# Stage 2 of a two-layer cross-attention kernel: the two folding steps of a pair are placed beside its products, and the output bias is added on VectorE

## The chip, the cores and the metric

One core of a Trainium2 chip runs the whole program. The metric is the device time in microseconds (us), the median over executions of one build; lower is better. Engine names are those of the profile: PE is the matrix engine (TensorE), PEld its weight loads, DVE is VectorE, ACT is ScalarE, POOL is GpSimd, SP is the sync engine, which here issues most of the DMAs.

## The reference

Two cross-attention layers follow one another over x, 4 x 1024 tokens of width 1024, with a context of 64 rows for each batch. Everything is float32.

```python
# layer 0: 32 heads of 32, 8 key/value heads, post-norm
q = x @ Wq + bq;  k = ctx @ Wk + bk;  v = ctx @ Wv + bv
attn = softmax(q k / sqrt(32) + mask)
x1 = layernorm((attn v) @ Wo + bo + x) * gamma + beta
# layer 1: 16 heads of 64
a = layernorm(ctx);  Q = x1 @ Wq1.T;  K = a @ Wk1.T;  V = a @ Wv1.T
y = x1 + tanh(gate) * (softmax(Q K / 8, masked) V) @ Wo1.T
```

Layer 1 has only 64 keys for each batch, so the kernel folds its weights: for each batch and head, Wq1 and K become one matrix `ad` (1024 x 1024, queries straight to scores), and V and Wo1 become one matrix `bd` (probabilities straight to the output).

## The kernel before, in words

The work goes in stages. Stage 1 makes layer 0's queries, scores, softmax and head outputs, and folds `ad`. **Stage 2**, which the change touches, multiplies the head outputs by Wo (`w_o`), adds the residual x and the bias bo, normalizes, writes x1 to DRAM, and folds `bd` on the side. Stage 3 does layer 1 with the folded matrices.

Stage 2 runs over 16 pairs of 128-row tiles. Pair 0 is done at the end of stage 1; the loop over `pair in range(1, NPAIR)` does the others. The product of a pair (256 x 1024 times 1024 x 1024) is done by a seven-product scheme of Strassen's kind, in `products`. Its seven steps, by bank, left block and right block, are

- step 0: X, A11 B11; step 1: X, S2 T2; step 2: V, S3 T3; step 3: X, S1 T1; step 4: X, S4 B22; step 5: V, A22 N4; step 6: W, A12 B21.

X, V and W are PSUM banks of the pool `wx` (4 buffers). X gathers four products one after another and V two; after every product its bank, as it then stands, is added on DVE to a quarter of the pair's residual rows `r` (line 455). So step 1 may write to X only when the DVE add of step 0 has read it, and step 4 only after the add of step 3. A product has four matmuls of 128 x 128 by 128 x 512; each shows as two PE instructions, so a product is "x8". In the trace's names, step 0 is `wo_B,o`, step 1 `wo_T,S`, step 2 `wo_T,o`, steps 3 and 4 `wo_B,S`, step 5 `wo_N,o` and step 6 `wo_B,o` again.

`project(a, w, r, fill, ...)` runs the seven steps and, after each, `ceil(len(fill)/7)` functions of the list `fill`. Into `fill` go, for a pair:

- `close_rows(pair - 1, r)`: for each of the two 128-row tiles of the pair before: two `bn_stats` (line 292), `bn_aggr` and an add (297, 298) with a square root on ACT (299), a reciprocal and a `scalar_tensor_tensor` (302, 306), a second one (309), and the store of x1 (1053). That is 12 functions.
- for pairs 1 to 8, `folded_values(vT, wch, pair - 1)`: two functions `keys(0)` and `keys(1)`. With 12 functions ahead of them and two after each step, they come in program order after step 6; in pair 1, which has two more functions ahead and three after each step, after steps 4 and 5.
- for pairs 13 to 15, sums of layer 1's first weight and transposes of x1.

One `keys` function makes, for two batches, a part of `bd`:

```python
for n in range(2):
    banks = two()                       # one of two "big" buffers: two PSUM banks
    for e in range(2):                  # rows 0..63 and rows 64..127 of the array
        nc.tensor.matmul(banks[e], vT[q, c, sub_ap(bp)], wch[q, n*512:(n+1)*512], ...)   # L924
    for e in range(2):
        nc.scalar.activation(st[:, e, n*512:(n+1)*512], banks[e], AF.Copy, scale=tanh_gate)  # L929
# then two DMAs of st to bd on SP (L933)
```

So a `keys` function is four matmuls of 64 rows, in two couples e = 0 and e = 1 that lie on different halves of the array, or eight PE instructions ("x8"), and four ACT evictions of 128 x 512.

`load_outputs(pair + 1)` (line 942 on), called at the head of a pair's turn, loads the next pair's head outputs `o` and its two residual tiles `r` on SP, and adds bo to each `r` on POOL (line 958), ahead of all products of that pair. `left_out` (lines 429 to 432), called by `tail` ahead of step 5, makes the next pair's left blocks on DVE.

The order in which an engine runs its instructions is set when the program is built: a planner goes through them in the order of the code, but where an engine would stand idle it takes the next instruction in that order that it holds to be ready. The trace shows it: in pairs 2 to 8 the first matmul of step 2 (`wo_T,o` x2) runs ahead of step 1 (`wo_T,S` x8). `tc.keep_in_program_order` pins an instruction behind the one that was written before it for its engine; the first `bn_stats` of a tile is pinned so, behind the add of the step that comes before it in the code.

Of the kernel before, what the change touches and what calls it, by code (L numbers as in the profile page):

```python
# [11 lines left out]
ALU = mybir.AluOpType  # L12
# [59 lines left out]
def tile_two_cross_attentions(  # L72
# [25 lines left out]
    nc = tc.nc  # L98

    def sub_ap(t):  # L100
        return slice(t * P, (t + 1) * P)
# [15 lines left out]
    def wx():  # L117
        return ps_wx.tile([P, 512], F32, tag="wx", name="wx")
# [14 lines left out]
    def open_pool(stack, name, bufs, side="left"):  # L133
        return stack.enter_context(tc.tile_pool(name=name, bufs=bufs, side=side, reuse_waits="tile"))
# [68 lines left out]
    def right_weight(w, tag, name, turned=False):  # L203
        r, loads = right_loads(w, tag, name, turned)
        run(loads)
        return r, right_sums(r)

    def run(steps):
        for s in steps:
            s()  # L210
# [179 lines left out]
    def two():  # L390
        b = big()
        return [b[:, 0:512], b[:, 512:1024]]
# [42 lines left out]
    def products(a, w, r, bias=None, tail=None):  # L435

        fresh = set()
        banks = {}  # L440

        def product(name, s, m, first, last):
            if first:
                banks[name] = wx()
            for k in range(HK):
                nc.tensor.matmul(  # L446
                    banks[name], a[s][:, k, :], w[m][:, k, :],
                    start=first and k == 0, stop=last and k == HK - 1, skip_group_check=True,
                )

        def add(u, n, name):
            bank = banks[name]
            at = r[u][:, n * 512 : (n + 1) * 512]
            if bias is None or (u, n) in fresh:
                nc.vector.tensor_tensor(at, bank, at, ALU.add)  # L455
            else:
                fresh.add((u, n))
                at = at.rearrange("p (h s) -> p h s", s=S)
                nc.vector.tensor_tensor(  # L459
                    at, bank.rearrange("p (h s) -> p h s", s=S),  # L460
                    bias.unsqueeze(1).to_broadcast([P, 512 // S, S]), ALU.add,
                )

        def step(name, s, m, first, last, u, n):
            if s == "A22" and tail:
                tail()
            product(name, s, m, first, last)
            add(u, n, name)

        order = [  # L470
            ("X", "A11", "B11", True, False, 0, 0),
            ("X", "S2", "T2", False, False, 1, 0),
            ("V", "S3", "T3", True, False, 1, 1),
            ("X", "S1", "T1", False, False, 1, 1),
            ("X", "S4", "B22", False, True, 0, 1),
            ("V", "A22", "N4", False, True, 1, 0),
            ("W", "A12", "B21", True, True, 0, 0),
        ]
        return [lambda o=o: step(*o) for o in order]

    def project(a, w, r, fill, bias=None, tail=None):

        share = -(-len(fill) // 7)
        for step in products(a, w, r, bias, tail):
            step()
            for _ in range(min(share, len(fill))):
                fill.pop(0)()

# [371 lines left out]
    steps = query_steps(0, rows)  # L860
# [16 lines left out]
    def chunk(w, k, name):  # L877
        t = wpool.tile([P, H], F32, tag="wb", name=f"{name}_{k}")
        nc.sync.dma_start(out=t, in_=w[sub_ap(k), :])
        return t  # L880
# [34 lines left out]
    def folded_values(vT, wch, c):  # L915


        def keys(bp):
            st = wpool.tile([P, 2, H], F32, tag="wb", name=f"b_{c}_{bp}")
            for n in range(2):  # L920
                banks = two()
                for e in range(2):
                    q = slice(e * S, (e + 1) * S)
                    nc.tensor.matmul(  # L924
                        banks[e], vT[q, c, sub_ap(bp)], wch[q, n * 512 : (n + 1) * 512],
                        start=True, stop=True,
                    )
                for e in range(2):
                    nc.scalar.activation(  # L929
                        st[:, e, n * 512 : (n + 1) * 512], banks[e], AF.Copy, scale=tanh_gate[:, 0:1]  # L930
                    )
            for b2 in range(2):
                nc.sync.dma_start(  # L933
                    out=bd[bp * 2 + b2, sub_ap(c), :].rearrange("(e s) o -> s e o", e=2),
                    in_=st[b2 * S : (b2 + 1) * S],
                )

        return [lambda bp=bp: keys(bp) for bp in range(2)]

    def load_o(pair, pool, tag="o2"):  # L940
        o = pool.tile([P, KC, 2 * P], F32, tag=tag, name=f"o2_{pair}")
        load = nc.sync.dma_start(out=o, in_=oTd[pair])
        if pair < 2:
            tc.keep_in_program_order(load)
        return o

    def load_outputs(pair):
        o = load_o(pair, o2pool) if pair > 1 else second if pair else load_o(0, early)
        r = []
        for u in range(2):  # L950
            t = pair * 2 + u
            ru = (rpool.tile([P, H], F32, tag="r", name=f"r_{t}") if pair
                  else early.tile([P, H], F32, tag="r", name=f"r_{t}", bufs=2))
            load = nc.sync.dma_start(out=ru, in_=x[sub_ap(t), :])
            if not pair:
                tc.keep_in_program_order(load)
            if pair:
                nc.gpsimd.tensor_tensor(ru, ru, bo_sb, ALU.add)  # L958
            r.append(ru)
        return o, r  # L960

# [86 lines left out]
    vT = fold.tile([P, KC, B * S], F32, tag="kvT", name="vT")  # L1048
    nc.sync.dma_start(out=vT, in_=vTd)

    def close_rows(pair, r):
        def last(u):
            nc.sync.dma_start(out=x1[pair][sub_ap(u), :], in_=r[u])

        steps = []
        for u in range(2):
            steps += normalize_steps(
                r[u], EPS0, f"0_{pair * 2 + u}", True, (gamma0_sb, beta0_sb)
            ) + [lambda u=u: last(u)]
        return steps  # L1060
# [3 lines left out]
    def load_x1(pair):  # L1064
        xq = xqpool.tile([P, 2 * NQ, QW], F32, tag="xq", name=f"xq1_{pair}")
        load_quarters(xq, x1[pair])
        return xq

    def turn_x1(pair, xq, pool=None, tag="xT"):
# [11 lines left out]
    wch = chunk(wo1, 0, "wo1")  # L1081
# [7 lines left out]
    values()  # L1089
    open_stage()  # L1090
    _, ahead_r = load_outputs(1)
    run(first)

    fill = [
        lambda u=u: nc.vector.tensor_tensor(first_rows[u], first_rows[u], bo_sb, ALU.add) for u in range(2)
    ]
    fill += close_rows(0, first_rows)
    for pair in range(1, NPAIR):
        r, a = ahead_r, ahead_a
        if pair + 1 < NPAIR:  # L1100
            ahead_o, ahead_r = load_outputs(pair + 1)
        if pair <= KC:
            ahead_w = chunk(wo1, pair, "wo1") if pair < KC else None
            fill += folded_values(vT, wch, pair - 1)
            wch = ahead_w
        if pair == KC + 2:
            w_a, w_a_sums = right_weight(ad[0], "wb", "a0", True)
        if pair in (NPAIR - 3, NPAIR - 2):
            fill += w_a_sums[0:2] if pair == NPAIR - 3 else w_a_sums[2:4]
        if pair == 3:  # L1110
            early_cm.close()
            xTpool = open_pool(last_cm, "x1T", 1)
            lxpool = open_pool(last_cm, "leftx", 1)
            xqpool = open_pool(last_cm, "x1q", 1)
        if pair == NPAIR - 4:
            xq = load_x1(1)
        if pair == NPAIR - 3:
            fill += turn_x1(1, xq)

        def tail():  # L1120
            nonlocal ahead_a
            if pair + 1 < NPAIR:
                ahead_a = left_out(ahead_o, lpool, f"0_{pair + 1}")
            else:
                turned[2]()

        project(a, w_o, r, fill, tail=tail)
        fill = close_rows(pair, r)
        if pair == NPAIR - 2:
            xq = load_x1(0)  # L1130
            turned = turn_x1(0, xq, o2pool, "o2")
            fill = turned[:2] + fill
# [78 lines left out]
    for pair in range(NPAIR):  # L1211
        r = []
        for u in range(2):
            ru = rpool.tile([P, H], F32, tag="r", name=f"r1_{pair}_{u}")
            nc.sync.dma_start(out=ru, in_=x1[pair][sub_ap(u), :])
            r.append(ru)
        fill = []
# [79 lines left out]
```

## Time and profile before

| | us |
|---|---|
| median of 3 runs | 1914.9 (1913.46 to 1915.07) |
| the profiled execution's own time | 1915.11 |
| its span, first to last instruction | 1913.3 |
| stage 2's loop, first product of pair 1 to first product of stage 3 | 719.8 to 1130.0 |
| PE busy over the span | 1868.9 (98%) |
| DVE / ACT / POOL busy | 1292.1 (68%) / 427.9 (22%) / 179.1 (9%) |
| the 30 adds of bo on POOL (line 958) | 78.5, mean 2.625 each |
| the two adds of bo on DVE, for pair 0 (line 1095) | 2.5, mean 1.226 each |
| a DVE add of a bank to `r` (line 455) | 0.686 |
| an ACT eviction of `keys` (line 929) | 0.687 |

Start times in the trace are microseconds from the span's start. The time outside the span is 1.8 us. "x8" in a line of the timeline is a run of eight instructions of one kind, with the time that they cover; "[0.97 <-DVE r L455]" behind a line is how long the engine stood idle before it and what ended that. The times of PE runs overlap a little, so that the distance from one start to the next is the better measure of what a run costs.

### The profile page before, as it was taken

How to read it: one execution, taken by the hardware profiler on the slowest of the kernel's cores; microseconds unless marked ns; L12 is line 12 of the kernel's file. 1: busy time of each engine (PE TensorE's matmuls, PEld its weight loads, DVE VectorE, ACT ScalarE, POOL GpSimd, SP SyncE). 2: the span in 40 equal slices, each digit the busy share in tenths (PEclk: the TensorE clock that was granted, in tenths of full speed). 3: DMA queues.
4: the chain of work that ended last, by engine and by line, in shares of the span. 5: the costliest groups of instructions: out<-in, count | busy, mean ns of one | idle time of the engine just before them, and what ended most of it. 6: DMA issues, size and time to landing. Idle time of an engine off the chain costs nothing.

```text
span 1913.3 us, 17522 instructions
## 1 busy us (share of the span) xinstructions
PE 1868.9 (98%) x6096; PEld 880.0 (46%) x6096; DVE 1292.1 (68%) x1582; ACT 427.9 (22%) x1396; POOL 179.1 (9%) x212
## 2 busy tenths in 40 slices
PE   8999999999998899999999999999999999999999
PEld 7744444444455653343344444444444444444444
DVE  3425589789878985575568778557665766576653
ACT  1101575666536751212100001000000000000000
POOL 0016011111100103121113100000000000000000
PEclk9999999999999899999999999999999999999999
DMA  8996599899878966567473363466656565657421
GB/s 276 184 222 192 158 253 247 253 252 261 252 186 275 302 234 207 188 207 238 164 218 138 121 141 90 110 165 158 150 143 165 150 158 143 165 142 165 121 88 44
DMA packets 220745, 350.54 MB, mean 183 GB/s; under 512 B 26992, under 2 KB 146160, under 8 KB 215664
## 3 DMA queue, kind: packets, MB, share of 16 engines
q1 hardware_dynamic: 152896, 242.44, 45.8%
q0 software_dynamic: 15216, 60.83, 10.5%
q10 hardware_dynamic: 52544, 46.14, 8.8%
q8 instruction: 48, 0.79, 0.2%
q14 instruction: 41, 0.34, 0.1%
HBM read 207.53 MB, written 141.82 MB: 183 GB/s over the span
## 4 chain that ended last, share of the span: by engine, by line
PE 82%; DVE 8%; DMA 5%; issue 2%; ACT 2%; POOL 0%; SPq 0%; DVEq 0%; POOLq 0%; ACTq 0%
PE wx L446 59%; PE wx L576 14%; PE big L680 2%; DMA pq<-p 2%; PE big L924 1%; PE wx L379 1%; PE big L379 1%; DVE s L684 1%; PE big L759 1%; DMA p<-s 1%; DMA q<-qTd 1%; DVE s L715 1%; DVE mx L691 1%; DVE sm L711 1%; DMA o<-oTd 1%
## 5 line engine op out<-in xcount | busy, mean ns | idle before, releaser
L455 DVE TENSOR_TENSOR r<-wx,r 128x512 f32<-128x512 f32 x224 | 153.5, 686 | 230.1 <-PE wx L446 215.3
L698 ACT ACTIVATE s<-s,mx 128x64 f32<-128x64 f32 x488 | 162.8, 335 | 74.9 <-DVE mx L691 70.7
L502 ACT ACTIVATE s<-s 128x1024 f32<-128x1024 f32 x32 | 33.7, 1057 | 651.7 <-DVE s L501 651.7
L459 DVE TENSOR_TENSOR s<-wx,key_bias 128x512 f32<-128x512 f32 x64 | 44.1, 690 | 136.7 <-PE wx L446 136.7
L446 PE MATMUL wx<-wo_B,S 128*128 128x512 f32 x256 | 117.1, 600 | 1.5 <-DVE r L455 1.5
L576 PE MATMUL wx<-xT,wq_S 128*128 128x512 f32 x256 | 116.5, 598 | 0.8 <-ACT z L587 0.8
L446 PE MATMUL wx<-b_B,pT 128*128 128x512 f32 x256 | 115.8, 593 | 0.6 <-ACT pT L414 0.6
L446 PE MATMUL wx<-b_B,S_p 128*128 128x512 f32 x256 | 116.0, 596 | 0.0
L446 PE MATMUL wx<-a_B,xT 128*128 128x512 f32 x256 | 115.4, 592 | 0.0
L446 PE MATMUL wx<-a_B,S_x 128*128 128x512 f32 x256 | 115.3, 593 | 0.1
L576 PE MATMUL wx<-xB,wq_A 128*128 128x512 f32 x256 | 115.1, 597 | 0.0
L446 PE MATMUL wx<-wo_B,o 128*128 128x512 f32 x256 | 114.8, 596 | 0.0
L958 POOL TENSOR_TENSOR r<-r,bo 128x1024 f32<-128x1024 f32 x30 | 78.5, 2625 | 313.8 <-DMA r<-in_x_dram 159.4
L684 DVE TENSOR_TENSOR s<-big,m 128x1024 f32<-128x1024 f32 x64 | 77.4, 1215 | 28.4 <-PE big L680 26.8
L680 PEld LDWEIGHTS big<-kv,q 64*128 64x128 f32 x1024 | 71.1, 195 | 48.3 <-issue 39.9
L698 ACT ACTIVATION_READ_ACCUMULATOR s<-s,mx 128x1 f32 x488 | 91.4, 187 | 0.0
L680 PE MATMUL big<-kv,q 64*128 64x128 f32 x1024 | 82.6, 292 | 2.6 <-DMA q<-qTd 2.6
L419 DVE STREAM_TRANSPOSE pT<-pq 128x1024 f32<-128x1024 f32 x66 | 78.0, 1219 | 3.3 <-DMA pq<-p 3.3
L446 PEld LDWEIGHTS wx<-wo_B,S 128*128 128x128 f32 x256 | 47.1, 190 | 67.7 <-issue 51.2
L715 DVE TENSOR_TENSOR s<-s,sm 128x1024 f32<-128x1024 f32 x64 | 77.0, 1216 | 0.9
L446 PEld LDWEIGHTS wx<-wo_B,o 128*128 128x128 f32 x256 | 47.8, 190 | 63.5 <-issue 62.3
L446 PEld LDWEIGHTS wx<-a_B,S_x 128*128 128x128 f32 x256 | 48.5, 190 | 62.0 <-issue 58.4
(162 smaller groups left out, 2903.5 us busy)
## 6 DMA issues: line engine op xcount, KB each, us to landing
p<-s POOLq DMA_DIRECT2D x19, 1024.0 KB, 8.1
pq<-p POOLq DMA_DIRECT2D x76, 256.0 KB, 6.0
xq<-in_x_dram SPq DMA_DIRECT2D x64, 256.0 KB, 10.2
q<-qTd SPq DMA_DIRECT2D x32, 512.0 KB, 7.4
oTd<-oT ACTq DMA_DIRECT2D x32, 512.0 KB, 7.4
ad<-a POOLq DMA_DIRECT2D x16, 1024.0 KB, 8.9
o<-oTd SPq DMA_DIRECT2D x16, 1024.0 KB, 5.1
r<-in_x_dram SPq DMA_DIRECT2D x32, 512.0 KB, 5.3
```

The costliest lines, as they stand in the source:

```text
L379: nc.tensor.matmul(ps[:, 0:256], w[k // HK, c // HK][:, k % HK, sub_ap(c % HK)], ct[:, k, :], start=(k == 0), stop=(k == KC - 1),)
L419: return nc.vector.transpose(dst.rearrange("p k (u i) -> p k u i", i=Q), t[:, :, k0 * Q : k1 * Q].rearrange("p u (k j) -> p k u j", j=Q),)
L446: nc.tensor.matmul(banks[name], a[s][:, k, :], w[m][:, k, :], start=first and k == 0, stop=last and k == HK - 1, skip_group_check=True,)
L455: nc.vector.tensor_tensor(at, bank, at, ALU.add)
L459: nc.vector.tensor_tensor(at, bank.rearrange("p (h s) -> p h s", s=S), bias.unsqueeze(1).to_broadcast([P, 512 // S, S]), ALU.add,)
L502: nc.scalar.activation(s, s, AF.Exp)
L576: nc.tensor.matmul(bank, w_q[a][:, k, sub_ap(i)], rows[b][:, k, :], start=first and k == 0, stop=last and k == HK - 1, skip_group_check=True,)
L680: nc.tensor.matmul(ps[:, at : at + P], q[on, c * 4 + g, :], k0bd[on, b, c, :], start=True, stop=True,)
L684: nc.vector.tensor_tensor(quarters[:, :, c * 8 : (c + 1) * 8], ps.rearrange("p (k a l) -> p a k l", a=NQ, l=Q), mask.rearrange("p e (h l) ...
L698: nc.scalar.activation(heads[:, e, k], heads[:, e, k], AF.Exp, bias=mx[:, e, k : k + 1], accum_out=sm[:, e, k : k + 1],)
L715: nc.vector.tensor_tensor(heads[:, e], heads[:, e], wide(sm[:, e]), ALU.mult)
L958: nc.gpsimd.tensor_tensor(ru, ru, bo_sb, ALU.add)
```

## The change

1. The functions of `folded_values` leave `fill`. `project` takes a table `beside`, from the index of a step to a function, and calls it right after that step, ahead of the functions of `fill`. `keys(0)` is called after step 1, `keys(1)` after step 4, in pairs 1 to 8.
2. The adds of bo on POOL in `load_outputs` are gone. Instead `close_rows` begins with two DVE adds of bo, one for each tile, after all products of the pair have been added to `r`; the two that pair 0 had already on DVE are now these.

`fill` so has 14 functions in nearly every pair (two after each step). The first `bn_stats` of the first tile now comes in the code after step 1, that of the second after step 4 (before, after steps 0 and 3).

```diff
-    def project(a, w, r, fill, bias=None, tail=None):
+    def project(a, w, r, fill, bias=None, tail=None, beside={}):
         share = -(-len(fill) // 7)
-        for step in products(a, w, r, bias, tail):
+        for i, step in enumerate(products(a, w, r, bias, tail)):
             step()
+            if i in beside:
+                beside[i]()
             for _ in range(min(share, len(fill))):
                 fill.pop(0)()
...
-            if pair:
-                nc.gpsimd.tensor_tensor(ru, ru, bo_sb, ALU.add)
...
-        steps = []
+        steps = [lambda u=u: nc.vector.tensor_tensor(r[u], r[u], bo_sb, ALU.add) for u in range(2)]
...
-    fill = [
-        lambda u=u: nc.vector.tensor_tensor(first_rows[u], first_rows[u], bo_sb, ALU.add) for u in range(2)
-    ]
-    fill += close_rows(0, first_rows)
+    fill = close_rows(0, first_rows)
...
+        beside = {}
...
-            fill += folded_values(vT, wch, pair - 1)
+            beside = dict(zip((1, 4), folded_values(vT, wch, pair - 1)))
...
-        project(a, w_o, r, fill, tail=tail)
+        project(a, w_o, r, fill, tail=tail, beside=beside)
```

## The prediction

> **What bounds the kernel now.** I read the page first: its busy times, then the chain that ended last.
>
> ```profile
> PE 1868.9 (98%) x6096; PEld 880.0 (46%) x6096; DVE 1292.1 (68%) x1582; ACT 427.9 (22%) x1396; POOL 179.1 (9%) x212
> ...
> PE 82%; DVE 8%; DMA 5%; issue 2%; ACT 2%; POOL 0%; SPq 0%; DVEq 0%; POOLq 0%; ACTq 0%
> ```
>
> PE holds the end almost everywhere, so the question in stage 2 is what lies between two products on PE. Next, the timeline of PE over one pair (pair 4; pairs 2 to 8 are alike).
>
> ```profile
> 809.32 3.70 PE L446 MATMUL wx<-wo_B,o 128*128 128x512 f32 x8
> 812.85 1.02 PE L446 MATMUL wx<-wo_T,o 128*128 128x512 f32 x2
> 813.86 3.70 PE L446 MATMUL wx<-wo_T,S 128*128 128x512 f32 x8
> 817.39 2.74 PE L446 MATMUL wx<-wo_T,o 128*128 128x512 f32 x6
> 819.97 3.60 PE L446 MATMUL wx<-wo_B,S 128*128 128x512 f32 x8
> 823.40 1.02 PE L446 MATMUL wx<-wo_N,o 128*128 128x512 f32 x2
> 824.35 3.70 PE L446 MATMUL wx<-wo_B,S 128*128 128x512 f32 x8
> 827.88 2.74 PE L446 MATMUL wx<-wo_N,o 128*128 128x512 f32 x6
> 830.46 3.60 PE L446 MATMUL wx<-wo_B,o 128*128 128x512 f32 x8
> 833.99 1.99 PE L924 MATMUL big<-wo,vT 64*128 64x512 f32 x8
> 836.53 2.28 PE L924 MATMUL big<-wo,vT 64*128 64x512 f32 x8 [0.56 <-ACT b L929]
> ```
>
> The next pair starts at 838.74, so the pair takes 29.42 us. Two things are to be seen. First, the two `keys` steps together take 838.74 - 833.99 = 4.75 us, because the second waits for ACT to empty the two big buffers. Second, between steps 0 and 1 and between steps 3 and 4 X is being read by DVE, and each such **gap** lasts 1.01 or 0.95 us (812.85 to 813.86, 823.40 to 824.35). It is not idle: the planner has put the first matmul of the next product there (x2, worth 2 x 0.43 = 0.86), and that product is short by it later (x6, 2.58).
>
> Third, pair 1, the one place of the trace where a `keys` step is written right behind step 4, as the change writes both.
>
> ```profile
> 731.43 3.60 PE L446 MATMUL wx<-wo_B,S 128*128 128x512 f32 x8
> 734.95 1.12 PE L924 MATMUL big<-wo,vT 64*128 64x512 f32 x2
> 736.01 3.70 PE L446 MATMUL wx<-wo_B,S 128*128 128x512 f32 x8
> 739.64 1.98 PE L924 MATMUL big<-wo,vT 64*128 64x512 f32 x6
> 741.55 3.70 PE L446 MATMUL wx<-wo_N,o 128*128 128x512 f32 x8
> 745.18 1.99 PE L924 MATMUL big<-wo,vT 64*128 64x512 f32 x8
> ```
>
> Here the gap was filled with the first matmul of `keys(0)`, as it is the next in the code, and step 5 has all its eight instructions afterwards. What is left of `keys(0)` (x6) takes 741.55 - 739.64 = 1.91 us, while a whole `keys` step takes the same: 747.10 (the next PE row) - 745.18 = 1.92. Six cost what eight cost because the halves e = 0 and e = 1 run side by side: in the whole step each half has four instructions at 0.43; with one matmul of half 0 gone, half 1 still has four. **A matmul of `keys` in the gap saves nothing, one of a product saves 0.86 us.**
>
> Fourth, the timeline of all engines at a POOL add.
>
> ```profile
> 1062.89 2.35 POOL L958 TENSOR_TENSOR r<-r,bo 128x1024 f32<-128x1024 f32 x1 [12.87 <-DVE r L306]
> 1062.94 3.38 DVE L309 SCALAR_TENSOR_TENSOR r<-r,rstd,beta 128x1024 f32<-128x1024 f32 x1
> ...
> 1066.98 3.27 PE L446 MATMUL wx<-wo_B,S 128*128 128x512 f32 x7 [0.63 <-DVE r L455]
> ```
>
> A DVE instruction that takes 1.28 us elsewhere takes 3.38 beside the POOL add, and here PE waits for the add queued behind it.
>
> **The change, part by part.** *The `keys` steps, pairs 2 to 8.* Removed: 4.75 us at the end of the pair, of which about 0.9 is waiting for ACT. Added, by pair 1's rows: step 0 before a `keys` matmul 3.52 (734.95 - 731.43), gap 1.06 (736.01 - 734.95), step 1 3.63, x6 1.91, step 2 whole 3.54 (as 779.92 to 783.46, a product after `keys`), then the same again for steps 3, 4, `keys(1)` and 5, and step 6 3.44: 2 x (3.52 + 1.06 + 3.63 + 1.91 + 3.54) + 3.44 = 30.76. Before, the seven pairs from 750.53 to 956.41 took 29.41 each. So +1.35 a pair, **+9.4 us** for seven. The bounds: if both gaps keep a product's matmul and both `keys` steps run whole, a pair is 3.44 + 1.01 + 3.63 + 1.92 + 2.6 + 3.43 + 0.95 + 3.63 + 1.92 + 2.6 + 3.44 = 28.57, or -0.84 (-5.9 in seven); if a gap takes both matmuls of one couple, the rest is x4, some 1.06 instead of 1.91, and with both gaps so the pair is 29.06 (-0.35). I take 30.76, as the row it rests on is the same code at the same place.
>
> ACT has its four evictions 0.7 us apart after the second half of each `keys` step (2.42 us in pair 1), then 10 us until the next: no wait for a buffer is left. The square root of line 299 may queue behind them for up to 2.4 us; DVE waits for it, and the adds that matter are those of steps 0 and 3, several us later. The four DMAs to bd go on SP as before, two after each `keys`; SP is in order, and behind them stand the stores of x1 and the loads of `o` and `r`. They take 5.4 us for four (837.66), now 2.7 twice. The load of `o` goes out when step 6 frees its buffer (834.09) and is used 20.7 us later (854.83); that distance is five products and two `keys` after as before. `r`, landed 5.2 us after its issue, has no POOL add behind it any more and waits for nothing new. Step 6 of the pair before must end, then DVE's store of x1 (one step later in the code) before a buffer of `r` is free; 6 buffers are three pairs, so this has over 20 us.
>
> *Pair 1.* It took 750.53 - 719.79 = 30.74 with one step split already and a wait of 0.97 at 725.31, behind a POOL add (DVE 724.57, idle 1.80 <-POOL). That wait goes (`r` landed at 721.9, step 0 ends at 723.3), the second split comes: 30.76, **0**. With the wait left it would be +1.
>
> *bo off POOL.* 30 adds of 2.625 us leave POOL, where nothing is queued behind them, and 30 of 1.226 come to DVE, 2.45 us a pair. DVE was busy 16.9 of 29.4 us in pairs 5 and 6, so there is room. The place that counts is ahead of step 0's add: the adds of bo can start after step 6's add, and in pairs without `keys` DVE stood idle 2.80 us there (before 984.68, 1009.17 and 1059.33). 2.45 fits with 0.35 to spare, and one of the two can go a product earlier. I take 0; if it doesn't fit, see rival 3. The lock goes: PE's step 3 came 0.59, 0.58 and 0.79 us late in pairs 11 to 13 (starts of 1016.62, 1041.61 and 1066.98 against the x6 before them plus 2.58), each behind a DVE instruction stretched by POOL: **-2.0 us**. DVE is nearly full there (31.2 of 32.0 us from 1009 to 1041, stretches included), so up to +1.5 may come back; 0 to be gained elsewhere, because other stretched instructions held up no product. In these pairs the first `bn_stats` now comes after step 1's add and the second tile's after step 4's, so DVE's long chain ends near the add of step 3; that is the +1.5.
>
> The Trainium skill, SBUF — State Buffer, section "Who interferes with whom", says that a DVE instruction with two SBUF inputs and a GpSimd instruction that reads SBUF lock each other out for a whole instruction. The 3.38 beside 2.35 agrees. By that rule alone DVE would get all of its lost time back; by the rows only three stretches reach PE.
>
> TensorEngine Tiling (Array Packing), section "Key Properties", says that a change of tiling mode drains the engine, which speaks against spreading: the two `keys` steps now stand in four places, not one. The rows have the price as about 0.1 us at each change (3.52 against 3.43), and it is in the sum. The page gives no time for it.
>
> *The end of stage 2.* Pair 15's closing runs beside the first scores, DVE busy without a break from 1130 to 1143. It becomes 2.45 us longer, but PE fills there with x4 runs of later products. 0, at most +2.
>
> **Sum**: +9.4 + 0 - 2.0 = +7.4 on the profiled 1915.1, or 1922.5. The profiled execution is 0.2 above the median of the runs, so this stands for the median too.
>
> **Rivals.**
> 1. *One gap of two is filled by a couple* (DVE's new adds make step 0's add later, the planner sees it and puts both halves there). The pair is 30.76 - 0.85 = 29.91, +0.5; 3.5 - 2.0 gives **1916.6**. For it: DVE is fuller ahead of step 0. Against: the filler was x2 in every gap of pairs 1 to 10.
> 2. *The other side: the `keys` steps run whole and the products keep the gaps.* Then the wait for ACT goes and nothing is lost: -5.9 - 2.0, **1907**. It decides if the planner holds the `keys` matmul not ready in the gap (its weights' chunk or its buffer late), so that step 2's or 5's comes first. For it: the gaps of pairs 2 to 8. Against: there no `keys` step was next in the code; where one was, it was taken.
> 3. *A new wait*: an add of bo starts just ahead of the end of step 0 and the add of step 0, which frees X, waits for it, up to 1.2 us in 15 pairs. On average half of it, +9: **1932**. Against: 2.80 against 2.45.
>
> **Chances.** Forecast 0.69, rival 1 0.11, rival 2 0.14, rival 3 0.06. The range takes the forecast with its bounds (+1 for pair 1, +1.5, +2 and a little of rival 3) and rival 1 with 2 us either way: 1914 to 1928, some 0.8. A measurement of this kernel can tell about 0.2% (3.8 us) from no change. Faster by more is rival 2 with rival 1's best corner, 0.15; within, rival 1 with a mixed forecast, 0.12; slower 0.73.
>
> **What would show it.** In the PE timeline of a pair 2 to 8: `big` x2 in both gaps, x6 after steps 1 and 4, steps 2 and 5 as x8, and 30.8 us from pair to pair. Line 306 and 309 means near 1.28 instead of 1.46 and 1.52, and no PE wait near 1016, 1042 and 1067. ACT's evictions never ahead of a PE wait. The prediction is wrong if the gaps hold x2 of a product or x4 or x8 of `keys`, or if DVE's add of step 0 starts more than 0.3 us after step 0.

## The result, and the profile after

The changed kernel takes 1919.8 us (median of 6 runs, 1917.13 to 1921.85), the kernel before 1914.6 (6 runs, 1913.14 to 1915.49). The ratio is 1.0026, with a 95% interval of 1.0014 to 1.0039: **slower by 5.2 us**. The profiled execution took 1920.84, its span is 1919.1. So the spans of the two profiled executions differ by 5.8 us.

The page's busy times and the chain that ended last, of the changed kernel:

```profile
PE 1881.0 (98%) x6096; PEld 881.9 (46%) x6096; DVE 1303.2 (68%) x1612; ACT 427.2 (22%) x1396; POOL 100.6 (5%) x182
...
PE 85%; DVE 7%; DMA 4%; issue 1%; ACT 1%; POOL 0%; DVEq 0%; SPq 0%; POOLq 0%; ACTq 0%
```

On the chain, PE has 85% where it had 82, ACT and issue 1 each where they had 2: waits went, and the time still grew. POOL lost its 78.5 us of adds and DVE has 30 instructions more. PE runs the same 6096 instructions and is busy 12.1 us longer, so no work was added to it: the same instructions lie less favourably. How is seen in the timeline of PE over half a pair of the changed kernel (pair 3; pairs 2, 5, 6, 7 and 8 look the same; columns: start, time covered, line, tiles, size, count):

```profile
785.58 1.12 PE L927 MATMUL big<-wo,vT 64*128 64x512 f32 x2
786.63 3.70 PE L446 MATMUL wx<-wo_T,S 128*128 128x512 f32 x8
790.26 1.98 PE L927 MATMUL big<-wo,vT 64*128 64x512 f32 x6
792.17 3.70 PE L446 MATMUL wx<-wo_T,o 128*128 128x512 f32 x8
795.71 3.60 PE L446 MATMUL wx<-wo_B,S 128*128 128x512 f32 x8
```

The gap between steps 0 and 1 (785.58 to 786.63) now holds the first matmul of `keys(0)`. The rest of that function, x6, still takes 1.91 us (792.17 - 790.26), and step 2 is whole, x8, 3.54. The wait of `keys(1)` for ACT, 0.56 before, is gone.

The other thing to be seen is DVE. Groups by shape, stage 2 of the changed kernel (busy us, mean ns | idle before):

```profile
L306 DVE SCALAR_TENSOR_TENSOR r<-r,mv,gamma 128x1024 f32<-128x1024 f32 x31 | 39.5, 1275 | 0.0
L1056 DVE TENSOR_TENSOR r<-r,bo 128x1024 f32<-128x1024 f32 x32 | 39.1, 1222 | 0.8
L309 DVE SCALAR_TENSOR_TENSOR r<-r,rstd,beta 128x1024 f32<-128x1024 f32 x30 | 38.5, 1282 | 0.7
```

The same view of the kernel before has, for lines 309 and 306:

```profile
L309 DVE SCALAR_TENSOR_TENSOR r<-r,rstd,beta 128x1024 f32<-128x1024 f32 x31 | 47.5, 1532 | 0.6
L306 DVE SCALAR_TENSOR_TENSOR r<-r,mv,gamma 128x1024 f32<-128x1024 f32 x31 | 45.3, 1460 | 0.0
```

Lines 306 and 309 fell from 1460 and 1532 ns to 1275 and 1282, since no POOL instruction lies beside them any more. The 32 adds of bo cost DVE 39.1 us.

To find where 5.8 us come from, I cut both spans at the first product of pairs 1, 2 and 9 and of stage 3:

| us | before | after | difference |
|---|---|---|---|
| ahead of pair 1 | 719.79 | 720.45 | +0.66 |
| pair 1 | 30.74 | 30.85 | +0.11 |
| pairs 2 to 8 | 205.88 | 214.41 | +8.53 |
| pairs 9 to 15 | 173.55 | 170.15 | -3.40 |
| stage 3 to the end | 783.34 | 783.24 | -0.10 |

In six of pairs 2 to 8 the changed kernel takes 30.75 us; in pair 4 it takes 29.91. **The pairs with `keys` lose 8.5 us, the pairs without win 3.4 back.**

### The profile page after: what moved, and what is told of

Read it like the earlier page. It is cut to its first block, busy times and chain, and to the rows that moved or that the text cites. A ratio compares the mean times of both kernels' runs of the same rounds, so it can differ in the third digit from the quotient of the medians.

```text
span 1919.1 us, 17488 instructions
## 1 busy us (share of the span) xinstructions
PE 1881.0 (98%) x6096; PEld 881.9 (46%) x6096; DVE 1303.2 (68%) x1612; ACT 427.2 (22%) x1396; POOL 100.6 (5%) x182
## 4 chain that ended last, share of the span: by engine, by line
PE 85%; DVE 7%; DMA 4%; issue 1%; ACT 1%; POOL 0%; DVEq 0%; SPq 0%; POOLq 0%; ACTq 0%
PE wx L446 61%; PE wx L579 14%; PE big L927 2%; PE big L683 2%; PE wx L379 1%; PE big L379 1%; DVE s L687 1%; PE big L762 1%; DMA p<-s 1%; DVE mx L694 1%; DVE s L718 1%; DMA pq<-p 1%; DMA q<-qTd 1%; DMA o<-oTd 1%; DVE sm L714 1%
## 5 line engine op out<-in xcount | busy, mean ns | idle before, releaser
L932 ACT ACTIVATE b<-big,tanh_gate 128x512 f32<-128x512 f32 x64 | 39.7, 682 | 198.8 <-PE big L927 122.6
L446 PEld LDWEIGHTS wx<-a_B,xT 128*128 128x128 f32 x256 | 48.6, 190 | 61.2 <-issue 60.5
```

The source lines that it names most:

```text
L446: nc.tensor.matmul(banks[name], a[s][:, k, :], w[m][:, k, :], start=first and k == 0, stop=last and k == HK - 1, skip_group_check=True,)
L932: nc.scalar.activation(st[:, e, n * 512 : (n + 1) * 512], banks[e], AF.Copy, scale=tanh_gate[:, 0:1])
```

## The experiments

**The theories.** *Filler theory* (mine): the loss is that a matmul of `keys` takes the place of a product's matmul in the gap, and that half of a couple taken alone saves nothing later. Then the loss hangs on which instruction is next in program order when the gap opens, and not on the steps being apart. *Spreading theory*: the loss is that the 64-row matmuls stand in four places between the products instead of in one. *DVE theory*: the loss comes from bo on DVE, or from the statistics that begin later. Ten kernels tell them apart. Each edit is given against the changed kernel, each ratio is to the kernel before as it ran alongside, and "stage" is the time from pair 1's first product to stage 3's in one profiled execution (410.17 before, 415.41 after).

**1. The steps alone.** bo goes back to POOL. Pair 0's two adds stay on DVE, as in the kernel before; the lines for that are left out here.

```diff
+            if pair:
+                nc.gpsimd.tensor_tensor(ru, ru, bo_sb, ALU.add)
...
-        steps = [lambda u=u: nc.vector.tensor_tensor(r[u], r[u], bo_sb, ALU.add) for u in range(2)]
+        steps = []
...
```

> The two keys steps beside steps 1 and 4, the bias left on POOL as before. Filler theory (a keys matmul in the gap takes the place of a product's and saves nothing): pairs 2 to 8 at 30.75 us each as in the changed kernel, pairs 9 to 15 at 173.5 us as before, +8.6 to +9.5 us against before, about 1923.7. DVE theory (what made the changed kernel slower is the bias on DVE and the later statistics): within 2 us of before, 1913 to 1916.

Measured: 1925.9 us, ratio 1.0062 (1.0050 to 1.0075). Pairs 2 to 8 take 214.41, as in the changed kernel, so the 8.5 us belong to the place of the steps and not to bo. The total came out some 2 us above the expectation: pairs 9 to 15 took 175.60, not the 173.55 of before, and pair 1 31.41. The reason is POOL, as rows of POOL, DVE and PE from the timeline of 1021 to 1028 show (the last row is cut at the window's end):

```profile
1022.28 6.83 POOL L961 TENSOR_TENSOR r<-r,bo 128x1024 f32<-128x1024 f32 x2 [23.29 <-DMA r<-in_x_dram]
...
1022.58 4.32 DVE L185 TENSOR_TENSOR a_T<-a_T,a_B 128x2048 f32<-128x2048 f32 x1
...
1027.56 0.70 PE L446 MATMUL wx<-wo_B,S 128*128 128x512 f32 x1 [1.21 <-DVE rstd L298]
```

A DVE instruction of 2.29 us is stretched to 4.32 beside the POOL adds, the add of step 3 comes only at 1026.82, and PE stands idle for 1.21. Where the stretches fall, and how many of them reach PE, changes with the order: in pairs 9 to 15 there are five such waits here, and there were three before.

**2. bo alone.** Both `keys` functions go back behind step 6.

```diff
-            beside = dict(zip((1, 4), folded_values(vT, wch, pair - 1)))
+            both = folded_values(vT, wch, pair - 1)
+            beside = {6: lambda both=both: run(both)}
```

> The bias on DVE, both keys steps together after step 6 in pairs 1 to 8. Filler theory: pairs 2 to 8 at 29.4 us as before, pair 1 also 29.4 instead of 30.7, pairs 9 to 15 at 170.2 us as in the changed kernel (-3.4): 1909.5 to 1911. DVE theory: slower than before, 1917 or more.

Measured: 1916.3 us, 1.0012 (1.0003 to 1.0021). Pairs 2 to 8 are back at 205.79, or 29.40 a pair: the DVE theory falls for those pairs. The total lies between the two forecasts, as pairs 9 to 15 took 176.50 where I expected 170.2, a gain over the 173.55 of before. Nearly all of that is one place, shown by the timeline of DVE and PE:

```profile
1031.39 1.22 DVE L1056 TENSOR_TENSOR r<-r,bo 128x1024 f32<-128x1024 f32 x1
...
1032.52 2.29 DVE L186 TENSOR_TENSOR a_N<-a_B,a_T 128x2048 f32<-128x2048 f32 x1
...
1036.79 2.07 PE L446 MATMUL wx<-wo_T,o 128*128 128x512 f32 x2 [4.48 <-DVE o L431]
```

DVE is full: an add of bo and a sum of layer 1's weight go ahead of `left_out` (lines 429 to 431), and PE, which needs these left blocks for the next pair, stands idle for 4.48 us. Afterwards it runs at a lower clock (last section). The changed kernel's 170.15 is 6.35 us shorter, and this place is 6.0 of it: 4.48, an x2 that took 1.05 too long (2.07 for 1.02) and an x8 that took 0.49 too long (4.19 for 3.70). So bo on DVE has a cost after all, but not one in every pair: it comes at once, where DVE has no room.

**3. The `keys` matmuls pinned** after steps 1 and 4, so that the planner cannot take them into the gap.

```diff
-                    nc.tensor.matmul(
+                    tc.keep_in_program_order(nc.tensor.matmul(
...
-                    )
+                    ))
```

> The changed kernel, with the matmuls of a keys step pinned behind the product that is written before them, so that none can go into a gap; the steps stay beside steps 1 and 4. Filler theory: the gaps hold a product's matmul again, a pair of 2 to 8 takes 28.6 us, pair 1 as well, pairs 9 to 15 170.2: -5.7 - 2.1 - 3.4, about 1903.5. Spreading theory (the price is the change between 64-row and 128-row work in four places instead of two, and the steps standing apart): no change of the places, so 1918 to 1920 as the changed kernel.

Measured: 1903.7 us, 0.9948 (0.9935 to 0.9962). The PE timeline of a pair of this kernel:

```profile
781.58 1.02 PE L446 MATMUL wx<-wo_T,o 128*128 128x512 f32 x2
782.52 3.70 PE L446 MATMUL wx<-wo_T,S 128*128 128x512 f32 x8
786.15 1.99 PE L927 MATMUL big<-wo,vT 64*128 64x512 f32 x8
788.07 2.84 PE L446 MATMUL wx<-wo_T,o 128*128 128x512 f32 x6
```

The `keys` matmuls stand at the same places of the code as in the changed kernel, as far apart, with the same adds on DVE. Only the gap has its product's matmul (x2) again, and step 2 is x6. Six of pairs 2 to 8 take 28.65 each, 2.10 less than after; the figure was 28.57 in my second rival. So the steps' standing apart is not the loss. On PE, though, the 64-row work now stands in two places of a pair and not in four, so this run alone doesn't say what the four places cost; edit 8 does.

**4 and 5. The steps in the gaps, and away from them.** One kernel calls `keys` after steps 0 and 3, by this edit; the other has (2, 5) at the same place.

```diff
-            beside = dict(zip((1, 4), folded_values(vT, wch, pair - 1)))
+            beside = dict(zip((0, 3), folded_values(vT, wch, pair - 1)))
```

> The changed kernel with the keys steps called after steps 0 and 3, so that a whole step of eight instructions lies in each gap. Filler theory: both halves of the array work in the gap, 1.92 us of keys work covers the wait of 1.0 us whole and no product is split; a pair takes 7 x 3.43 + 2 x 1.92 + 0.2 to 0.4, 28.1 to 28.3 us, -8.4 for pairs 2 to 8, -2.5 for pair 1, -3.4 for pairs 9 to 15: about 1900.5. Spreading theory: as the changed kernel, 1918 to 1920.

> The changed kernel with the keys steps called after steps 2 and 5, behind which no gap lies. Filler theory: the gaps hold a product's matmul, the keys steps run whole, 28.6 us a pair in pairs 1 to 8 as with the pinned steps, 170 us in pairs 9 to 15: 1902 to 1906. Spreading theory: as the changed kernel.

Measured: in the gaps **1902.4 us, 0.9935 (0.9923 to 0.9948)**, the fastest of all; away from them 1904.3, 0.9944 (0.9929 to 0.9959). The PE timeline of the first:

```profile
779.19 1.99 PE L927 MATMUL big<-wo,vT 64*128 64x512 f32 x8
781.11 3.70 PE L446 MATMUL wx<-wo_T,S 128*128 128x512 f32 x8
784.64 3.60 PE L446 MATMUL wx<-wo_T,o 128*128 128x512 f32 x8
```

The whole function, 1.92 us, now lies where the gap was, so PE waits for nothing and the products need no filler: step 2 is x8 again, and the pair still takes only 28.26. Away from the gaps it is 28.65, as with the pin. Pairs 9 to 15 have one wait behind line 431 in both of these, 1.61 us away from the gaps and 0.68 with the pin.

**6. No bias.** The adds of bo go from DVE and stand nowhere else.

```diff
-        steps = [lambda u=u: nc.vector.tensor_tensor(r[u], r[u], bo_sb, ALU.add) for u in range(2)]
+        steps = []
```

> The changed kernel without the 32 adds of bo (the bias is left out of the result). If the adds lie wholly under PE's work, as the prediction had it: pairs 2 to 8 at 30.7 us, pairs 9 to 15 at 170 us, the time of the changed kernel within 1 us. DVE theory (its new adds are part of the loss): 3 us or more faster than the changed kernel.

Measured: 1921.1 us, 1.0034 (1.0021 to 1.0047); the stage takes 416.51, not less than the 415.41 with the adds (pairs 2 to 8 214.40, 9 to 15 170.99). With two functions fewer in `fill` the statistics also begin a step earlier again, as before the change, so neither part of the DVE theory holds the loss. In the changed kernel's order the 39.1 us of adds on DVE lie beside products and cost nothing that can be measured.

**7. One step in the gap.** `keys(0)` stays after step 1, `keys(1)` goes after step 5.

```diff
-            beside = dict(zip((1, 4), folded_values(vT, wch, pair - 1)))
+            beside = dict(zip((1, 5), folded_values(vT, wch, pair - 1)))
```

> Half a dose: the changed kernel with keys(0) after step 1 as there and keys(1) after step 5, behind which no gap lies. Filler theory: the loss is so much for each gap, so a pair of 1 to 8 takes the middle of 30.75 and 28.62, 29.7 us; 8 pairs x 1.06 = 8.5 us below the changed kernel, about 1911.5, with one x2 and x6 of keys and one whole x8 in each pair. If the loss were one of the place of both steps together, it would be 1904 or 1920.

Measured: 1914.0 us, 0.9996 (0.9987 to 1.0006). A pair (all but pair 4) takes 29.70, half way from 30.75 to 28.65, so the loss is one of so much a gap, 1.05. The total missed the expectation by 2.5 us, 1.6 of which is a wait of PE behind line 431 at 1035.73.

**8. Whole couples.** Each `keys` function is cut in its two couples; one couple is called after each of the steps 0, 1, 3 and 4.

```diff
...
-        return [lambda bp=bp: keys(bp) for bp in range(2)]
+        return [lambda bp=bp, n=n: keys(bp, n) for bp in range(2) for n in range(2)]
...
-            beside = dict(zip((1, 4), folded_values(vT, wch, pair - 1)))
+            beside = dict(zip((0, 1, 3, 4), folded_values(vT, wch, pair - 1)))
```

> The changed kernel with each keys step cut into its two couples of matmuls, called after steps 0, 1, 3 and 4, so that each gap holds both halves of one couple and the other couple follows the next product. Filler theory: x4 in the gap, x4 of some 1.06 us afterwards instead of x6 of 1.91; 29.0 us a pair instead of 30.75, 1.7 x 8 = 14 us below the changed kernel, about 1906. Spreading theory: the 64-row work stands in four places of a pair as in the changed kernel (x2, x6, x2, x6 there), so no change, 1918 to 1920.

Measured: 1906.4 us, 0.9959 (0.9945 to 0.9972). The PE timeline of a pair:

```profile
808.55 1.13 PE L931 MATMUL big<-wo,vT 64*128 64x512 f32 x4
809.61 3.70 PE L446 MATMUL wx<-wo_T,S 128*128 128x512 f32 x8
813.24 1.13 PE L931 MATMUL big<-wo,vT 64*128 64x512 f32 x4
814.30 3.70 PE L446 MATMUL wx<-wo_T,o 128*128 128x512 f32 x8
```

This is the plainest test of the theory. In the changed kernel the gap holds x2 and the rest, x6, costs 1.91; here the gap holds x4, twice as many instructions in the same 1.06 us, and the rest costs 1.06. The pair is 29.06, which is my figure for it, and the 64-row work stands in four places of a pair on PE, as in the changed kernel: the spreading theory is refuted. The second x4 lies in no gap and takes 1.06 us (814.30 - 813.24), where four instructions one after another would take 4 x 0.43 = 1.72. **The two halves of a couple run side by side.**

**9. Together, no bias.** Edits 2 and 6 at once.

```diff
-        steps = [lambda u=u: nc.vector.tensor_tensor(r[u], r[u], bo_sb, ALU.add) for u in range(2)]
+        steps = []
...
-            beside = dict(zip((1, 4), folded_values(vT, wch, pair - 1)))
+            both = folded_values(vT, wch, pair - 1)
+            beside = {6: lambda both=both: run(both)}
```

> The kernel with both keys steps after step 6 and without any add of bo (the bias is left out of the result). In the kernel with the bias alone moved, PE stood still for 4.5 us at 1032, behind a VectorE that had been busy without a break. If that stall came of VectorE's 2.45 us more a pair, it is gone here: pairs 9 to 15 at 170 us, about 1909. If it came of something else (a late load of o, the order of the store of x1), it stays, and the time is 1914 to 1916.

Measured: 1915.6 us, 1.0006 (0.9997 to 1.0015). Pairs 9 to 15 took 170.90, as expected, where edit 2 alone had 176.50: the stall of edit 2 comes from the adds of bo. The total missed the expectation by over 6 us, because of a new wait in pair 1 (34.20 instead of 29.39 in edit 2). DVE ran line 306 of pair 0's first tile at 726.27 (731.09 in edit 2), came to line 309 and waited for the load of `beta`, which SP issues at 727.44:

```profile
731.78 1.28 DVE L309 SCALAR_TENSOR_TENSOR r<-r,rstd,beta 128x1024 f32<-128x1024 f32 x1 [4.15 <-DMA beta<-in_beta_dram]
...
733.72 5.40 PE L446 MATMUL wx<-wo_B,S 128*128 128x512 f32 x8 [2.86 <-DVE r L455]
```

**10. In the gaps, bo on POOL.** Edit 4 with edit 1, whose lines for pair 0 are left out here too.

```diff
+            if pair:
+                nc.gpsimd.tensor_tensor(ru, ru, bo_sb, ALU.add)
...
-        steps = [lambda u=u: nc.vector.tensor_tensor(r[u], r[u], bo_sb, ALU.add) for u in range(2)]
+        steps = []
...
-            beside = dict(zip((1, 4), folded_values(vT, wch, pair - 1)))
+            beside = dict(zip((0, 3), folded_values(vT, wch, pair - 1)))
```

> The keys steps after steps 0 and 3, the bias back on POOL: what the second part of the change is worth where the first does no harm. If POOL's hold on VectorE's instructions reaches PE (as at 1016, 1041 and 1067 of the kernel before), pairs 9 to 15 take 173.5 to 176 us instead of 170.1 and the kernel is 3 to 6 us slower than with the bias on VectorE (1905.5 to 1908.5 against 1902.4). If the difference seen so far is only the planner's other order, it is within 2 us of it either way.

Measured: 1904.8 us, 0.9954 (0.9942 to 0.9967). Pairs 9 to 15 take 174.51 instead of the 170.07 of edit 4, with four waits of PE behind DVE, 1.27 the longest; pairs 2 to 8 hardly differ (198.57 with one wait of 0.66, 197.84 without). The stage is 5.2 us longer than in edit 4, all but 0.7 of it in the pairs where POOL's hold was expected to show. The medians are only 2.4 apart, between the two forecasts, and their intervals against the kernel before overlap; the runs of one kernel spread over up to 6 us.

**Put together**, medians in us:

| `keys` called | bo on POOL | bo on DVE | bo left out |
|---|---|---|---|
| both after step 6 | 1914.6 (before) | 1916.3 | 1915.6 |
| after steps 1 and 4 | 1925.9 | 1919.8 (after) | 1921.1 |
| after steps 0 and 3 | 1904.8 | 1902.4 | |

In the kernel before, `keys` of pair 1 come after steps 4 and 5. The kernels ran on several occasions, on which the kernel before had medians of 1913.4 to 1914.6, so a difference in the table is good to one or two us. Down a column stands what the place of the steps is worth: with bo on POOL, +11 and -10 us against both after step 6. Along a row stands what moving bo to DVE is worth: +1.6, -6.1 and -2.4, so it depends on where the steps are. The change's own loss is thus the sum of a place that costs some 11, of which 8.5 lie in pairs 2 to 8 and most of the rest in the stretches by POOL that edit 1 shows, and a move of bo that brings back some 6.

## Why the prediction was right

It was slower, as forecast, by 5.2 us instead of 7.4. The steps of stage 2 add up to as much in the two traces, 8.53 + 0.11 - 3.40 = 5.24, and both large terms came out below the forecast, so that no error hid another. By its steps:

- **The `keys` steps, pairs 2 to 8: +9.4 forecast, +8.53 measured.** The mechanism is shown by edit 3, which keeps the steps where they are in the code and changes what the gap holds, and by edit 8, which keeps the four places on PE and fills the gap with a whole couple. A pair of 30.76 was forecast, and six of seven took 30.75. The seventh, pair 4, is rival 1 in one of its gaps: its second gap holds a whole couple (x4 at 829.99 and x4 at 834.68), and 30.76 - 0.85 = 29.91 is what it took.
- **Pair 1: 0 forecast, +0.11 measured.** The wait behind POOL (0.97) went and the second split came.
- **bo off POOL, pairs 9 to 15: -2.0 forecast, -3.40 measured.** This is the term that was mis-sized. The three waits that I counted went: their pairs had taken 25.00, 25.17 and 25.37 us where an undisturbed one took 24.47, 2.1 in all. What I put at "0 to be gained elsewhere" was the other 1.3. All seven pairs now take 24.13 to 24.42. Rows of DVE and PE in pair 13 show one of the ways:

```profile
1066.36 1.21 DVE L1056 TENSOR_TENSOR r<-r,bo 128x1024 f32<-128x1024 f32 x1
...
1066.52 1.88 PE L446 MATMUL wx<-wo_T,o 128*128 128x512 f32 x4
1067.49 0.68 DVE L455 TENSOR_TENSOR r<-wx,r 128x512 f32<-128x512 f32 x1
...
1068.23 3.69 PE L446 MATMUL wx<-wo_T,S 128*128 128x512 f32 x8
```

  Here an add of bo runs just ahead of the add of step 0, so DVE reads X 0.97 us late (1067.49 - 1066.52), the gap is 1.71 us, and the planner has put two matmuls of the product into it, worth 4 x 0.43 = 1.72. Nothing is lost: a late add that the planner knows of is filled. I had counted on gaps of 1.01 alone, in which 0.15 stays empty. Pairs 11, 12, 13 and 15, in which a gap holds x4 or x6 of a product, took 24.23, 24.31, 24.13 and 24.23, together 1.0 less than four of 24.47. Why the gaps fall so in these pairs I did not work out.
- **"Up to +1.5 may come back" on a full DVE: nothing came back in the changed kernel, but the price was too low.** Where it did come, it was 0.7 (edit 3), 1.6 (edits 5 and 7) and some 6 (edit 2), and not at the add of step 3 but at `left_out`, which I had left out of the list of what queues on DVE. Rival 3's late add did arise, in pairs 13 and 15 (0.97 and 0.77 us late, an add of bo ahead of it both times), and cost nothing, because the planner filled the longer gap; its price, half of 1.2 in 15 pairs, was wrong.
- **The adds of bo hidden: right.** Edit 6 has none and isn't faster. **The wait for ACT: right**, no eviction lies ahead of a wait of PE. **The lock: right**, 1275 and 1282 ns against "near 1.28".
- **The end of stage 2: 0 forecast, -0.10 measured** from stage 3's first product on.
- Two signs that I had named as showing the prediction wrong did come up, in three of the 15 pairs: x4 of `keys` in one gap of pair 4, and the late adds of pairs 13 and 15. They leave the mechanism of the other pairs as it was, but the signs were drawn too strictly.
- Rival 2, whole `keys` and a product in the gaps, is what edit 3 makes on purpose: 28.65 a pair against 28.57 forecast. That the planner would not do so by itself was the point of the forecast, and it did not.

**What stays open.** The start of stage 2 moved between 717.7 and 721.7 us from kernel to kernel, though no edit touches the products ahead of it; that is as large as some of the differences here, and I didn't follow it up. Each stage time is from one profiled execution. And why `left_out` comes late in edits 2, 3, 5 and 7, and not in the changed kernel with the same work on DVE, was not tried. The traces show what runs ahead of it: the four sums of layer 1's weight, written with pairs 13 and 14, are taken ahead into pairs 10 to 12; in edit 2 the last of them stands in front of line 429, in edits 5 and 7 an add of bo stands between lines 429 and 430, and in the changed kernel lines 429 to 431 come with neither between them. Edit 3's short wait has no such row. What makes the planner choose one order or the other stays open.

## What to carry to other kernels

A filler in a gap is worth what it saves later, not what it fills: half of a couple that runs side by side saves nothing, so give the gap a whole couple, or the whole unit (1902.4 us against 1913.4 of before alongside), or pin it out of the gap. Where a planner fills gaps by program order, a line of code one step earlier or later can decide the sign: in pairs 2 to 8, after steps 1 and 4 it costs 8.5 us, after steps 0 and 3 it brings 8.0. And an engine that is free for 32% of the span can still be full where it counts: list all that queues on it in that stretch, not only the link that you have in mind.

## What the runs showed of the hardware

A wait of PE can cost more than itself. After the idle 4.48 us of edit 2 the granted clock (the column ahead of the DMA share and GB/s) was half, by the windows of that kernel:

```profile
1036.70:1038.70 2.00, 1.91 (x3) 0.83 (x4) 1.24 (x3) 0.00 (x0) 0.00 (x0) 0.50 0.99 404
1038.70:1040.70 2.00, 2.00 (x5) 0.98 (x4) 0.00 (x0) 0.00 (x0) 0.00 (x0) 0.71 0.37 152
1040.70:1042.70 2.00, 2.00 (x7) 0.81 (x6) 0.00 (x0) 0.00 (x0) 0.00 (x0) 1.00 0.00 0
```

The 0.71 is a mean: narrower windows have 0.50 from 1036.50 to 1039.80 and 1.00 from 1039.90 on, so the half clock lasted some 3 us after PE had started again at 1036.79. After 2.86 us without a matmul (3.69 without a weight load) in edit 9 the clock was 0.68 in the mean over the next 5.3 us, and an x8 took 5.40 instead of 3.70. There it was 1.00 from 733.72, where the matmuls started again, to 734.85, then 0.50 from 734.95 to 738.30 and 1.00 after that: the half clock set in more than 1 us after the work had come back. After 1.61 and 1.60 us in edits 5 and 7 it stayed at 1.00. The Trainium skill, TensorE: Matmul & The Clock Gate, section "What's actually happening", gives the half rate after an idle window of about 3.4 us that runs freely; 4.48 agrees, 1.6 agrees, and the 2.86 falls below its figure if only matmuls are counted.
